# Seven block products for the second linear of ten batches, its h in two loads, and the degrees one burst sooner

## The chip, the cores and the metric

The kernel runs on one core of one Trainium2 chip, as one program with one launch. The metric is the device time of that launch in microseconds (us). All data are float32. The core has five engines with queues of their own: TensorE (PE), VectorE (DVE), ScalarE (ACT), GpSimd (POOL) and SyncE (SP), which here only issues DMAs.

## The reference, cut to what matters

There are two layers over x of 16 batches, 1024 nodes and 256 channels. The first is an attention layer with a graph term; the second aggregates over the graph and applies two linears, each followed by a batch norm over all batches and nodes. The change is in the second linear of the second layer (512 features to 256) and, for one small step, in the node degrees.

```python
def _L1_gnn_ref(features, A, W1, b1, g1, be1, W2, b2, g2, be2):
    ...
    A_norm = A + jnp.eye(n, dtype=A.dtype)
    deg = jnp.sum(A_norm, axis=0) + jnp.sum(A_norm, axis=1) - jnp.diagonal(A_norm)
    dinv = jax.lax.rsqrt(deg)
    A_hat = A_norm * dinv[:, None] * dinv[None, :]
    agg = jnp.einsum('nm,bmd->bnd', A_hat, features)
    x = agg.reshape(-1, d)
    h = jax.nn.relu(_batchnorm(x @ W1.T + b1, g1, be1))
    out = h @ W2.T + b2
    out = _batchnorm(out, g2, be2)
    return out.reshape(b, n, -1)
x = _layernorm(x + _L0_gnn_ref(x, L0_gnn_para, adj, L0_gnn_kv_w), axis=-1)
x = _layernorm(x + _L1_gnn_ref(x, adj, L1_gnn_W1, ..., L1_gnn_be2), axis=-1)
```

## The kernel before

The kernel has four stages in order of time. The order of the work on PE, ACT and DVE is written out by hand in all four (the manual schedules opened at L1158 and L1321); the queues of SP and POOL are ordered by the framework's scheduler, and each is worked off in order.

1. Attention, to about 1698 us. It runs in units of one batch, one pair of heads, one half of the queries and 128 keys; two units make a burst, 16 bursts a batch. In the last batch, work of the second layer is hung on the bursts by their number, in the table `last` (L1193 to L1205): transposing the adjacency (bursts 0 to 7), `degrees` (L1095, burst 9), transposing the weights (10, 11), the first two scalings of the adjacency (12). `degrees` adds up row and column sums on DVE, takes the inverse root on POOL (L589), writes it to DRAM and loads it back as a row on all partitions (L1102, L1104, both in SP's queue). `scale_adjacency` (L1112, DVE) needs that row, and the running sums of the softmax (L955, L957) queue behind it on DVE.

2. Aggregation and the first linear, about 1698 to 2291 us. The products of blocks are made by seven multiplications instead of eight (`products`, L631): from blocks A11..A22 and B11..B22, four sums of the left blocks (`left_sums`, L685) and four of the right (`right_sums`, L691) are formed, and seven products p1, p6, p2, p7, p5, p4, p3 accumulate in three PSUM banks a, b and c. p1 is copied to SBUF by ACT (L650); p6 and p7 plus p1 give the sums u2 and u3 on DVE (L642 with a bias, L640 without); p2 completes output block 0 on ACT (L663); p5 plus u3 gives block 3 (L673), p4 in bank b plus p1 block 2 (L642), p3 in bank c plus u2 block 1 (L681), all on DVE. A bank is added to by a later product (p7 and p4 in b, p2 in a, p3 in c) only when it has been read after the earlier one. The result h (16 batches of 512 x 1024) goes to DRAM (L1415, L1506).

3. The second linear, 2291 to 2511 us, in 16 passes of one batch. `load_h` (L1531, SP) loads one h of 2 MB into one of two 16 KB-a-partition buffers (`hl`), two batches ahead: it starts when PE has finished with the batch whose buffer it takes. ACT applies batch norm and relu in place to the four 128 x 1024 blocks of the next batch (`scale_shift1`, L1482). PE makes 16 products per batch, two blocks of outputs c by four blocks of features k by two halves of the nodes (L1553); a float32 product of 128 x 512 stands in the profile as two matmul instructions. DVE adds the bias into `o2T` in SBUF, where all 16 outputs stay (L1580), and takes statistics of the PSUM tile (L1584). `batchnorm` (L1295) adds the bias to the mean afterwards.

4. The second batch norm, the residual, the layer norm and the output, 2511 to 2605 us. It loads the first layer's results again (`xf`): three batches into the pool `xp`, four into the pool `hl` in two pairs (`load_x1_pair`, L1602), and further ones as buffers come free.

Of the kernel before, what the change touches and what calls it, by code (L numbers as in the profile page):

```python
# [10 lines left out]
F32 = mybir.dt.float32  # L11
I32 = mybir.dt.int32
AF = mybir.ActivationFunctionType
ALU = mybir.AluOpType
# [4 lines left out]
P = 128  # L19
HALF = 512  # L20
# [495 lines left out]
def fast_path(  # L516
# [19 lines left out]
    nc = tc.nc  # L536
    B, N, C = x.shape
    H = 4
    D = C // H
    NCH = N // P  # L540
    CC = C // P
    FH = W1.shape[0]
    HC = FH // P
# [16 lines left out]
    def tile_s(name):  # L560
        return psum["s"].tile([P, N], F32, tag="s", name=name)
# [7 lines left out]
    x1_d = [dram.tile([P, NCH, C], F32, tag=f"x1_{b}", name=f"x1_{b}") for b in range(B)]  # L569
# [115 lines left out]
    def left_sums(eng, S, a11, a12, a21, a22):  # L685
        eng.tensor_tensor(S[0], a21, a22, ALU.add)
        eng.tensor_tensor(S[1], S[0], a11, ALU.subtract)
        eng.tensor_tensor(S[2], a11, a21, ALU.subtract)
        eng.tensor_tensor(S[3], a12, S[1], ALU.subtract)
# [12 lines left out]
    cols = {}  # L702
# [24 lines left out]
    with (  # L727
# [297 lines left out]
        def run(fs, k):  # L1025
            for f, a in fs[:k]:
                f(*a)
            del fs[:k]
# [129 lines left out]
        with tc.manual_schedule(engines={mybir.EngineType.PE, mybir.EngineType.Activation, mybir.EngineType.DVE}):  # L1158
# [33 lines left out]

            last = {u: [(transpose_adjacency, (u, h)) for h in (0, 1)] for u in range(NCH)}  # L1193
            for u, todo in (
                (1, (load_weights,)), (6, (load_x1l, 0)), (9, (degrees,)),
                (10, (transpose_weights, 0)), (11, (transpose_weights, 1)),
                (12, (add_identity,)), (12, (scale_adjacency, 0)), (12, (scale_adjacency, 1)),
            ):
                last.setdefault(u, []).append((todo[0], todo[1:]))
# [92 lines left out]

    w1T, w2T = wl["w1T"], wl["w2T"]

    def batchnorm(stats, gamma, beta, k, name, eng=nc.gpsimd, bias=None):  # L1295

        mv = const.tile([P, k, 2], F32, name=f"{name}_mv")
        sg = const.tile([P, k], F32, name=f"{name}_sg")  # L1300
        sh = const.tile([P, k], F32, name=f"{name}_sh")

        def coefficients(j):
            g, s = sg[:, j : j + 1], sh[:, j : j + 1]
            nc.vector.bn_aggr(mv[:, j, :], stats[:, j].rearrange("p a s -> p (a s)"))
            eng.tensor_scalar(g, mv[:, j, 1:2], EPS, None, ALU.add)
            rsqrt(g, g, 0.0)
            if bias is not None:
                eng.tensor_tensor(
                    mv[:, j, 0:1], mv[:, j, 0:1], bias[:, j : j + 1], ALU.add  # L1310
                )
            eng.tensor_tensor(g, g, gamma[:, j : j + 1], ALU.mult)
            eng.tensor_tensor(s, mv[:, j, 0:1], g, ALU.mult)
            eng.tensor_tensor(s, beta[:, j : j + 1], s, ALU.subtract)

        return coefficients, sg, sh
# [8 lines left out]
    with (  # L1325
# [6 lines left out]
        def bank(name):  # L1332
            return ps8.tile([P, HALF], F32, tag="bank", name=name)

        def temps(k):
            return lambda key, name: strt.tile([P, HALF], F32, tag=f"{key}{k}", name=f"{key}_{name}")
# [144 lines left out]
        def scale_shift1(h, k):  # L1481
            nc.scalar.activation(  # L1482
                h, h, AF.Relu, bias=sh1[:, k : k + 1], scale=sg1[:, k : k + 1]
            )
# [27 lines left out]

    with tc.tile_pool(name="hl", bufs=2) as hl, tc.tile_pool(name="o2p", bufs=1) as o2p:
        o2T = [
            o2p.tile([P, CC, N], F32, tag=f"o2_{b}", name=f"o2_{b}") for b in range(B)
        ]
# [3 lines left out]
        def load_x1(b, pool, tag):  # L1522
            xf[b] = pool.tile([P, NCH, C], F32, tag=tag, name=f"xf_{b}")
            nc.sync.dma_start(xf[b], x1_d[b])

        coefficients2, sg2, sh2 = batchnorm(
            bn2_st, cols["g2"], cols["be2"], CC, "bn2", nc.vector, cols["b2"]
        )
        hs_of = {0: h0}

        def load_h(b):  # L1531
            ht = hl.tile([P, HC, N], F32, tag="hl", name=f"hl_{b}")
            nc.sync.dma_start(ht, h_d[b])
            hs_of[b] = [ht[:, k, :] for k in range(HC)]

        load_h(1)
        for b in range(B):
            if b + 2 < B:
                load_h(b + 2)
            if b + 1 < B:  # L1540
                for k in range(HC):
                    scale_shift1(hs_of[b + 1][k], k)
            h = hs_of.pop(b)
            pss = [tile_s(f"po2_{b}_{c}") for c in range(CC if b < B - 1 else CC - 1)]
            last_ps = [tile_o(f"po2_last_{half}") for half in range(2 if b == B - 1 else 0)]

            def half_ps(c, hs):
                if last_ps and c == CC - 1:
                    return last_ps[0 if hs == H0 else 1]
                return pss[c][:, hs]  # L1550

            def mm(c, k, hs):
                nc.tensor.matmul(  # L1553
                    half_ps(c, hs), w2T[:, k, c * P : (c + 1) * P], h[k][:, hs],
                    start=(k == 0), stop=(k == HC - 1),
                )

            if b == 0:

                for ks in (range(HC // 2), range(HC // 2, HC)):  # L1560
                    for c in range(CC):
                        for k in ks:
                            for hs in (H0, H1):
                                mm(c, k, hs)
            for c in range(CC):
                last = b == B - 1 and c == CC - 1
                if b:
                    for k, hs in (
                        [(k, hs) for hs in (H0, H1) for k in range(HC)] if last
                        else [(k, hs) for k in range(HC) for hs in (H0, H1)]  # L1570
                    ):
                        mm(c, k, hs)
                if last:
                    for hs in (H0, H1):
                        nc.scalar.activation(
                            o2T[b][:, c, hs], half_ps(c, hs), AF.Identity,
                            bias=cols["b2"][:, c : c + 1],
                        )
                else:
                    nc.vector.tensor_scalar(  # L1580
                        o2T[b][:, c, :], pss[c], cols["b2"][:, c : c + 1], None, ALU.add
                    )
                for half, hs in enumerate((H0, H1)):
                    nc.vector.bn_stats(bn2_st[:, c, 2 * b + half, :], half_ps(c, hs))  # L1584
                if b == B - 1:
                    coefficients2(c)
            if b >= B - 3:
                load_x1(b - (B - 3), xp, "x")

# [6 lines left out]
        with (  # L1596
            tc.tile_pool(name="ps_held", bufs=3, space=PSUM) as ps_held,
            tc.tile_pool(name="ps_sum", bufs=2, space=PSUM) as ps_sum,
        ):
            pairs = {}  # L1600

            def load_x1_pair(b):  # L1602

                pairs[b] = hl.tile([P, 2, NCH, C], F32, tag="hl", name=f"xf_{b}_{b + 1}")
                for i in range(2):
                    xf[b + i] = pairs[b][:, i]
                    nc.sync.dma_start(xf[b + i], x1_d[b + i])

            load_x1_pair(3)
            load_x1_pair(5)  # L1610

            def scale_shift(b, cs=range(CC)):
                for c in cs:
# [72 lines left out]
            def finish(b, *coeffs):  # L1686
                xt, hx = xf.pop(b), held.pop(b)
                y = o2T[b].rearrange("p c n -> p (c n)").rearrange("p (n c) -> p n c", c=C)
                last = b == B - 1
                for n in (0, 1, 2, 3) if last else (0, 1):  # L1690
                    rstd, nmr = coeffs[n // 4]
                    nc.vector.tensor_scalar(
                        y[:, n, :], xt[:, n, :], rstd[:, n : n + 1], nmr[:, n : n + 1],
                        ALU.mult, ALU.add,
                    )
                for n in (4, 5, 6, 7) if last else (4, 5, 6, 7, 2, 3):
                    rstd, nmr = coeffs[n // 4]
                    nc.scalar.activation(
                        y[:, n, :], hx[:, (n - 4) * C : (n - 3) * C] if n >= 4 else xt[:, n, :],
                        AF.Identity, bias=nmr[:, n : n + 1], scale=rstd[:, n : n + 1],  # L1700
                    )
                dst = out[b].rearrange("(n p) c -> p n c", p=P)
                if last:
                    nc.sync.dma_start(dst[:, M0, :], y[:, M0, :])
                    nc.scalar.dma_start(dst[:, M1, :], y[:, M1, :])
                elif b >= B - 4:
                    nc.sync.dma_start(dst[:, M1, :], y[:, M1, :])
                    nc.sync.dma_start(dst[:, M0, :], y[:, M0, :])
                else:
                    nc.sync.dma_start(dst, y)  # L1710
                if b in (4, 6):
                    load_x1_pair(b + 6)
                elif b + 7 < B and not 3 <= b < 7:
                    load_x1(b + 7, xp, "x")

            add_x1(0, 2)
            add_x1(0, 3)
# [56 lines left out]
```

## Time and profile before

| | |
|---|---|
| runs | 2607.45, 2608.11, 2610.22 us, median 2608.11 |
| the profiled execution | 2607.23 us, of which 2605.1 us are the span of the core's instructions |
| PE busy | 2560.0 us, 98% of the span |
| DVE, ACT, POOL busy | 58%, 46%, 14% |
| granted TensorE clock | 0.998 |
| second linear, 2291.4 to 2511.3 us | PE busy throughout |

How to read it. The page gives the busy time of each engine, then the costliest groups of instructions: line of the kernel, engine, operation, tiles written and read, count, busy time and the mean duration of one, and behind the last bar how long the engine stood idle just before them and what ended that. A timeline gives start, duration and the same description for single instructions or runs of like ones; when its engine was idle before, the idle time and what ended it follow in brackets. The chain of waits is the sequence of work that ended last, followed back from the end. Consecutive instructions of an engine overlap at their edges, so the distance between two starts, and not the duration, says how fast a queue is worked off.

### The profile page before, as it was taken

Reading aid. Unit: us, or ns where it says so; the run is one execution under the profiler, and the core shown is the slowest. Engines: PE = TensorE matmul, PEld = TensorE weight load, DVE = VectorE, ACT = ScalarE, POOL = GpSimd, SP = SyncE. Lnnn points to the kernel's source line nnn. Section 1 sums busy time; section 2 is a strip of 40 time slices with the busy share of each in tenths; the row PEclk is TensorE's granted clock in tenths of the full one; section 3 lists DMA queues with packets and bytes.
Section 4 is the critical chain, followed back from the end, with each engine's and each line's share of the span. In section 5 each row is a group of like instructions: output and inputs, shape, how many; then the busy total and the mean of one; then the engine's idle time right before and its main releaser. Section 6 shows DMA issues by size and latency. Waiting matters only on the chain.

```text
span 2605.1 us, 32348 instructions
## 1 busy us (share of the span) xinstructions
PE 2560.0 (98%) x13158; PEld 1126.9 (43%) x13158; DVE 1515.6 (58%) x1974; ACT 1201.7 (46%) x1479; POOL 355.8 (14%) x420
## 2 busy tenths in 40 slices
PE   9999999999999999999999999999999999999997
PEld 4443443444434434444444344444444444444455
DVE  5375665655656556556565566675655656443368
ACT  6365564664655646646556464621101111043358
POOL 0010110101101001011010010232211222000026
PEclk9999999999999999999999999999999999999999
DMA  4001101011011010110110101022212222254449
GB/s 145 1 10 42 33 10 41 17 26 33 10 41 34 9 42 10 33 33 10 42 34 9 42 3 48 10 81 97 93 69 93 85 97 77 102 208 161 149 170 345
DMA packets 134622, 168.97 MB, mean 65 GB/s; under 512 B 86848, under 2 KB 120128, under 8 KB 124096
## 3 DMA queue, kind: packets, MB, share of 16 engines
q1 hardware_dynamic: 129104, 115.95, 14.4%
q0 software_dynamic: 4832, 50.34, 4.6%
q8 instruction: 105, 1.72, 0.3%
q10 hardware_dynamic: 528, 0.52, 0.1%
q14 instruction: 53, 0.43, 0.1%
HBM read 99.36 MB, written 67.44 MB: 64 GB/s over the span
## 4 chain that ended last, share of the span: by engine, by line
PE 86%; DVE 9%; ACT 3%; issue 1%; DMA 1%; POOL 0%; DVEq 0%; POOLq 0%; ACTq 0%
PE ps L926 16%; PE pg L829 16%; PE po L947 16%; PE po L1553 8%; PE pv L879 5%; PE b_agg L1371 4%; PE c_agg L1371 4%; PE pk L866 3%; PE a_agg L1371 2%; PE b_h L1403 2%; PE c_h L1403 2%; PE pxT L790 1%; PE a_h L1403 1%; PE den L977 1%; PE pagg L1139 1%; PE pg L851 1%
## 5 line engine op out<-in xcount | busy, mean ns | idle before, releaser
L931 ACT ACTIVATE p<-ps 128x1024 f32<-128x1024 f32 x512 | 496.8, 1024 | 186.0 <-PE ps L926 155.3
L957 DVE TENSOR_TENSOR acc<-acc,p 128x1024 f32<-128x1024 f32 x384 | 485.7, 1265 | 122.6 <-ACT p L931 94.1
L926 PE MATMUL ps<-qT,kT 64*64 64x512 f32 x4096 | 490.8, 592 | 0.7 <-DVE qT L838 0.3
L947 PE MATMUL po<-p,v 64*64 64x512 f32 x4096 | 488.2, 589 | 1.1 <-ACT p L931 1.1
L829 PE MATMUL pg<-wg,x 128*128 128x512 f32 x960 | 420.9, 594 | 0.0
L947 PEld LDWEIGHTS po<-p,v 64*64 64x64 f32 x4096 | 159.8, 133 | 281.7 <-issue 270.2
L1013 POOL TENSOR_TENSOR x<-x,o 128x512 f32<-128x512 f32 x64 | 122.2, 1909 | 1165.9 <-DVE o L1008 1165.9
L829 PEld LDWEIGHTS pg<-wg,x 128*128 128x128 f32 x960 | 178.9, 190 | 221.5 <-issue 208.5
L926 PEld LDWEIGHTS ps<-qT,kT 64*64 64x64 f32 x4096 | 152.0, 133 | 281.5 <-issue 250.2
L1553 PE MATMUL po<-hl,w12T 128*128 128x512 f32 x496 | 213.1, 592 | 0.8 <-ACT hw L1497 0.8
L838 DVE SCALAR_TENSOR_TENSOR qT<-pg,para_s 128x1024 f32<-128x1024 f32 (+1 forms) x34 | 39.2, 1161 | 238.2 <-PE pg L829 235.0
L819 DVE SCALAR_TENSOR_TENSOR wg<-wg,adj_s 128x1024 f32<-128x1024 f32 x128 | 162.1, 1278 | 19.6 <-ACT wg L815 19.6
L810 ACT ACTIVATE wg<-crow,ccol 128x1024 f32<-128x1024 f32 x128 | 147.2, 1150 | 6.5 <-DMA crow<-c 5.8
L1553 PEld LDWEIGHTS po<-hl,w12T 128*128 128x128 f32 x496 | 94.2, 190 | 119.8 <-issue 116.0
L815 ACT ACTIVATE wg<-wg 128x1024 f32<-128x1024 f32 x128 | 136.2, 1065 | 1.8
L1482 ACT ACTIVATE hl<-hl,bn_sh,bn_sg 128x1024 f32<-128x1024 f32 x64 | 74.1, 1228 | 132.7 <-DMA hl<-h 131.3
L879 PE MATMUL pv<-kvw_s,xT 128*128 128x256 f32 x512 | 126.8, 390 | 6.7 <-ACT kT L870 6.7
L965 DVE TENSOR_TENSOR oT<-po,oT 128x512 f32<-128x512 f32 x64 | 44.3, 692 | 145.8 <-ACT oT L964 145.8
L866 PE MATMUL pk<-xT,kvw_s 128*128 128x512 f32 x256 | 121.9, 598 | 3.3 <-ACT v L884 3.3
L1580 DVE TENSOR_SCALAR o<-po,col_b 128x1024 f32<-128x1024 f32 x31 | 39.8, 1284 | 136.8 <-PE po L1553 136.8
L624 ACT ACTIVATE x<-x,nm_l,rs_l 128x256 f32<-128x256 f32 x128 | 64.8, 587 | 110.3 <-POOL nm_l L620 110.3
L841 ACT ACTIVATE qT<-qT 128x1024 f32<-128x1024 f32 (+1 forms) x34 | 34.1, 1007 | 175.9 <-DVE qT L838 175.9
(182 smaller groups left out, 2759.1 us busy)
## 6 DMA issues: line engine op xcount, KB each, us to landing
h<-hw POOLq DMA_DIRECT2D x16, 2048.0 KB, 6.9
hl<-h SPq DMA_DIRECT2D x15, 2048.0 KB
x<-x POOLq DMA_DIRECT2D x16, 1024.0 KB, 4.2
x1l<-x SPq DMA_DIRECT2D x16, 1024.0 KB
xf<-x SPq DMA_DIRECT2D x16, 1024.0 KB
x<-in_x_dram SPq DMA_DIRECT2D x15, 1024.0 KB
out_dram<-o SPq DMA_DIRECT2D x12, 1024.0 KB
crow<-c SPq DMA_DIRECT2D x15, 512.0 KB
```

The source lines that it names most:

```text
L810: nc.scalar.activation(w, s["crow"], AF.Abs, bias=s["ccol"][:, n : n + 1])
L815: nc.scalar.activation(w, w, AF.Tanh, scale=0.5)
L819: nc.vector.scalar_tensor_tensor(w, w, 1.0, adj_s[:, n, :], op0=ALU.subtract, op1=ALU.mult)
L829: nc.tensor.matmul(s["pg"][:, hs], xt[:, n, c * P : (c + 1) * P], s["wg", n][:, hs], start=(n == 0), stop=(n == NCH - 1),)
L866: nc.tensor.matmul(ps, kvw_s[:, c, kc * P : (kc + 1) * P], s["xT"][:, c, hs], start=(c == 0), stop=(c == CC - 1),)
L879: nc.tensor.matmul(pt[:, j * C : (j + 1) * C], s["xT"][:, c, n * P : (n + 1) * P], kvw_s[:, c, C : 2 * C], start=(c == 0), stop=(c == CC - 1),
L926: nc.tensor.matmul(ps[kh * D : (kh + 1) * D, hd * HALF : (hd + 1) * HALF], kT[r, pr, ks], qT[r, pr, qh * HALF : (qh + 1) * HALF], start=Tr ...
L931: nc.scalar.activation(p, ps, AF.Exp)
L947: nc.tensor.matmul(g["po"][kh][hd * D : (hd + 1) * D, :], s["v"][r, m, h * D : (h + 1) * D], p[r, hd * HALF : (hd + 1) * HALF], start=(m = ...
L957: nc.vector.tensor_add(g["acc"], g["acc"], p)
L1371: nc.tensor.matmul(ps, left, right, start=(start and i == 0), stop=(i == NCH // 2 - 1), skip_group_check=True,)
L1553: nc.tensor.matmul(half_ps(c, hs), w2T[:, k, c * P : (c + 1) * P], h[k][:, hs], start=(k == 0), stop=(k == HC - 1),)
```

## The change

- Batches 1 to 10 of the second linear (`SEVEN`) go through `products` too. The left blocks are the blocks of W2 transposed, with sums `w2S` made once on POOL in a buffer of the pool `xp`; the right blocks are feature halves by node halves of h. Every product is two 128 x 128 by 128 x 512 matmuls (i = 0, 1). Batches 0 and 11 to 15 stay as they were.
- The four right sums of a batch, each of two 128 x 512 parts, are made on DVE (`h_sums`) in the space of the outputs of batches 12 to 15, which are not written yet; odd and even batches alternate. The temporaries p1, u2 and u3 lie in the space of the next batch's output.
- h comes in two loads of 1 MB, features k = 0, 2 and k = 1, 3, into four buffers of half the size; from batch 2 on, a load is one batch ahead in the program. ACT scales in the order 0, 2, 1, 3.
- The statistics are taken from `o2T`, with the bias in it, so `batchnorm` adds no bias.
- In the last stage four single loads take the place of the two pairs.
- `degrees` is hung on burst 8 of the last batch.

```diff
-                (1, (load_weights,)), (6, (load_x1l, 0)), (9, (degrees,)),
+                (1, (load_weights,)), (6, (load_x1l, 0)), (8, (degrees,)),
...
-            if bias is not None:
-                eng.tensor_tensor(
-                    mv[:, j, 0:1], mv[:, j, 0:1], bias[:, j : j + 1], ALU.add
-                )
...
-    with tc.tile_pool(name="hl", bufs=2) as hl, tc.tile_pool(name="o2p", bufs=1) as o2p:
+    with tc.tile_pool(name="hl", bufs=4) as hl, tc.tile_pool(name="o2p", bufs=1) as o2p:
...
         def load_h(b):
-            ht = hl.tile([P, HC, N], F32, tag="hl", name=f"hl_{b}")
-            nc.sync.dma_start(ht, h_d[b])
-            hs_of[b] = [ht[:, k, :] for k in range(HC)]
+            parts[b] = [hl.tile([P, 2, N], F32, tag="hl", name=f"hl_{b}_{i}") for i in range(2)]
+            for i in range(2):
+                nc.sync.dma_start(parts[b][i], h_d[b][:, i::2, :])
+            hs_of[b] = [parts[b][k % 2][:, k // 2, :] for k in range(HC)]
+        SEVEN = range(1, B - 5)
+        w2S = xp.tile([P, 4, 2, P], F32, tag="x", name="w2S")
+        K0, K1 = slice(0, HC // 2), slice(HC // 2, HC)
+        left_sums(
+            nc.gpsimd, [w2S[:, i] for i in range(4)],
+            w2T[:, K0, C0], w2T[:, K1, C0], w2T[:, K0, C1], w2T[:, K1, C1],
         )
+        def h_sums(b, i, later):
+            t = parts[b][i]
+            T = [o2T[B - 4 + 2 * (b % 2) + j // 2][:, i, (j % 2) * HALF : (j % 2 + 1) * HALF]
+                 for j in range(4)]
+            b11, b12, b21, b22 = t[:, 0, H0], t[:, 0, H1], t[:, 1, H0], t[:, 1, H1]
+            if not later:
+                nc.vector.tensor_tensor(T[0], b12, b11, ALU.subtract)
+                nc.vector.tensor_tensor(T[1], b22, T[0], ALU.subtract)
+            else:
+                nc.vector.tensor_tensor(T[2], b22, b12, ALU.subtract)
+                nc.vector.tensor_tensor(T[3], b21, T[1], ALU.subtract)
+        def linear2_seven(b):
+            X = parts[b]
...
+            def mm(k, ps, start):
+                for i in range(2):
+                    left, right = {
+                        1: (w2T[:, i, C0], X[i][:, 0, H0]),
+                        2: (w2T[:, 2 + i, C0], X[i][:, 1, H0]),
+                        3: (w2S[:, 3, i, :], X[i][:, 1, H1]),
+                        4: (w2T[:, 2 + i, C1], T(3, i)),
+                        5: (w2S[:, 0, i, :], T(0, i)),
+                        6: (w2S[:, 1, i, :], T(1, i)),
+                        7: (w2S[:, 2, i, :], T(2, i)),
+                    }[k]
+                    nc.tensor.matmul(
+                        ps, left, right, start=(start and i == 0), stop=(i == 1),
+                        skip_group_check=True,
+                    )
...
+            if b in SEVEN:
+                nxt = b + 1
+                if b > 1:
+                    load_h(nxt)
+                p1, p6, p2, p7, p5, p4, p3 = linear2_seven(b)
+                p1()
+                h_sums(b, 1, True)
+                run(rest, 1)
+                p6()
+                run(rest, 1)
+                p2()
+                run(rest, 1)
+                for k in (0, 2):
+                    scale_shift1(hs_of[nxt][k], k)
+                p7()
+                statistics2(b, 0)
+                p5()
+                for k in (1, 3):
+                    scale_shift1(hs_of[nxt][k], k)
+                if nxt in SEVEN:
+                    h_sums(nxt, 0, False)
+                p4()
+                if nxt in SEVEN:
+                    h_sums(nxt, 1, False)
+                p3()
+                if nxt in SEVEN:
+                    h_sums(nxt, 0, True)
+                rest = [(statistics2, (b, i)) for i in (3, 2, 1)]
+                if nxt not in SEVEN:
+                    run(rest, 3)
+                    load_h(nxt + 1)
+                continue
...
-                    nc.vector.bn_stats(bn2_st[:, c, 2 * b + half, :], half_ps(c, hs))
+                    nc.vector.bn_stats(bn2_st[:, c, 2 * b + half, :], o2T[b][:, c, hs])
...
+            if b == 0:
+                for i, later in ((0, False), (1, False), (0, True)):
+                    h_sums(1, i, later)
...
-            load_x1_pair(3)
-            load_x1_pair(5)
+            for b in range(3, 7):
+                load_x1(b, hl, "hl")
...
-                if b in (4, 6):
-                    load_x1_pair(b + 6)
-                elif b + 7 < B and not 3 <= b < 7:
-                    load_x1(b + 7, xp, "x")
+                if b + 7 < B:
+                    load_x1(b + 7, *((hl, "hl") if 3 <= b < 7 else (xp, "x")))
```

## The prediction, on record before the changed kernel ran

> **What bounds the kernel now.** I read the page's engine shares first, then the costliest groups.
>
> ```profile
> PE 2560.0 (98%) x13158; PEld 1126.9 (43%) x13158; DVE 1515.6 (58%) x1974; ACT 1201.7 (46%) x1479; POOL 355.8 (14%) x420
> ...
> L1553 PE MATMUL po<-hl,w12T 128*128 128x512 f32 x496 | 213.1, 592 | 0.8 <-ACT hw L1497 0.8
> ...
> L1482 ACT ACTIVATE hl<-hl,bn_sh,bn_sg 128x1024 f32<-128x1024 f32 x64 | 74.1, 1228 | 132.7 <-DMA hl<-h 131.3
> ```
>
> PE has almost no gaps. In the second linear 496 instructions took 213.1 us with 0.8 us idle before them: 0.4293 us each, or 0.8585 for a product (two instructions), 13.74 for a batch's 16. The time by stretches, asked for one batch, shows the others:
>
> ```profile
> 2401.30:2415.00 13.70, 13.70 (x33) 6.08 (x32) 4.97 (x6) 4.63 (x4) 0.00 (x0) 1.00 0.42 155
> ```
>
> Columns: stretch and length, busy PE, weight loads, DVE, ACT, POOL, clock, DMA share, GB/s. DVE and ACT are a third busy, POOL does nothing, DMA runs at 42%. So a product removed is worth its 0.86 us until DVE, which takes over much work, becomes the slower ring. The timelines of DVE price that work; the first fence is without POOL work, the second beside POOL's sums L686 to L689.
>
> ```profile
> 1716.47 0.68 DVE L696 TENSOR_TENSOR aT<-ahT,aT 128x512 f32<-128x512 f32 x1
> 1717.07 0.68 DVE L693 TENSOR_TENSOR aT<-ahT 128x512 f32<-128x512 f32 x1
> 1717.78 0.69 DVE L694 TENSOR_TENSOR aT<-ahT,aT 128x512 f32<-128x512 f32 x1
> 1718.39 0.68 DVE L695 TENSOR_TENSOR aT<-ahT,ahT 128x512 f32<-128x512 f32 x1
> ```
>
> ```profile
> 2131.77 1.64 DVE L694 TENSOR_TENSOR tT<-agg,tT 128x512 f32<-128x512 f32 x1
> 2133.33 1.75 DVE L695 TENSOR_TENSOR tT<-agg 128x512 f32<-128x512 f32 x1
> ```
>
> A free sum holds the queue for 0.605 us start to start (0.715 where the next one reads it: 1717.07 to 1717.78), a disturbed one for 1.6. How fast PE takes up after DVE:
>
> ```profile
> 1775.72 0.75 DVE L642 SCALAR_TENSOR_TENSOR u_h<-b_h,col_b,p_h 128x512 f32<-128x512 f32 x1 [0.28 <-ACT hw L663]
> ```
>
> ```profile
> 1776.53 1.12 PE L1403 MATMUL b_h<-tT,wS 128*128 128x512 f32 x2 [1.85 <-DVE u_h L642]
> 1777.49 3.60 PE L1371 MATMUL a_agg<-ahT,x1l 128*128 128x512 f32 x8
> ```
>
> The sum ended at 1776.47; the next product follows at 1777.49, one product (0.86) after 1776.63: 0.16 after the release. The other way, b_h started at 2124.51, its slot ended at 2125.37, and DVE read it at 2125.58: 0.21. Loads, from the timelines of SP and ACT:
>
> ```profile
> 2401.62 82.72 SPq L1533 DMA_DIRECT2D hl<-h  x7
> ```
>
> ```profile
> 2409.99 4.63 ACT L1482 ACTIVATE hl<-hl,bn_sh,bn_sg 128x1024 f32<-128x1024 f32 x4 [9.31 <-DMA hl<-h]
> ```
>
> A 2 MB load is issued 0.3 after PE leaves the buffer and used 8.4 later. For the degrees, the chain of waits:
>
> ```profile
> 1672.54 8.42 DMA dinv<-dg
> 1680.97 5.02 DMA dinv_row<-dinv
> ...
> 1696.15 1.03 ACT p L931
> 1697.23 1.09 PE po L947 x8
> ```
>
> [...]
>
> **The change part by part.**
>
> *PE.* Ten batches lose two products each: 20 x 0.8585 = 17.17 us off. At full pace a batch is 14 x 0.8585 = 12.02.
>
> *DVE's ring, batches 2 to 10.* Per batch DVE has eight sums, five reads of PSUM (L642 0.66 start to start, L673/L681 0.605) and four statistics (2.46 for four, so 0.595 each): 10.6 us with two dependent pairs. The order has waits, so I follow one turn from the start of u3 at t: u3 0.66 and a statistic fit before p5 is done, at t+1.72 (p5 follows p7 at once); block 3 0.605, two sums 1.32, block 2 0.66, two sums 1.32, block 1 0.605, four sums 2.42, a statistic 0.595: u2 starts at t+9.24, is there 0.75 later, PE starts p7 0.16 on, runs 1.72, and DVE sees it after 0.21: t+12.08. That is 0.06 over PE's 12.02; block 3 waits for two engines, which costs the first linear's u2 0.06 (0.27 instead of 0.21). I take 12.12, 0.1 over: nine batches +0.9. Bounds: 0 if PE sets the pace; +5 if every start is 0.64, on the way to L642's 0.66 (some ten sums and reads in the turn).
>
> *The first turn.* Six sums for batch 1 stand on DVE behind batch 0's last bias and statistics. With 0 at PE's end of batch 0: bias from 0.21, sums from 2.60; the two T1 end at 4.01 and 5.33. p6, due at 1.72, gets its first half going at 4.17 (2.45 late), the second at 5.49 (0.46 more). u2 waits behind four more sums until 7.66, ends at 8.41, and p7, due at 8.07, starts at 8.57: 0.50. Together +3.4.
>
> *Loads.* Half the bytes each. [...] DVE asks for the parts at 9.4 and 11.4: nothing. If both landed at 8.4, the second part's sums would slip from 11.4 to 13.1, and p7 by 1.8 in every second turn: 0.9 a batch, +8. On SP, xf_0 now stands behind both first h pairs; that queue waits for PE's end of batch 0 there as before. The last stage's single loads are issued no later than the pairs: nothing.
>
> *ACT.* 4 x 1.15 + 0.5 (L650) + 0.6 (L663) = 5.7 of 12.0, and p1's copy needs to be done one product later: hidden.
>
> *POOL.* w2S puts four ops ahead of the write of h 14: at wS's 1.02, 0.72, 1.70, 1.59 it is 5.0, from 2275.2 (PE's last read of the buffer) to 2280.3, and its next work before was at 2282.9: hidden; beyond that it would delay the batch-norm coefficients one for one.
>
> *Degrees.* On DVE they move ahead of two pairs of statistics and one sum of 128x1024: 1667.8 instead of 1670.0. The small DMA goes out once the three before it in SP's queue have, at 1671.5 instead of 1672.5: 1 us. DVE waited 0.97 for the row, and PE 1.11 for ACT behind DVE at 1697.23: 0.9 off; bounds 0 and 1.1.
>
> *Bias and statistics.* One 0.08 step less at the end: 0.1 off. Reading them from SBUF (0.675) or PSUM (0.685) is equal.
>
> Sum: -17.17 + 0.9 + 3.4 - 0.9 - 0.1 = -13.9. From the profiled execution (2607.23, of which 2605.1 are span): 2593.3. The median of the runs is 0.9 higher; I forecast **2594.2**.
>
> **The rivals.** *DVE dearer* (0.22): waits of sums on two engines cost starts; +1 to +6 on the forecast, about 2598. For it: the ring is already at its limit. *Loads land together* (0.10): 2594.2 + 8 = 2602. For it: both go down one queue at once, and DMA had 42% use[...]. *Slower* (0.08): the sums, in the stage's SBUF space and beside loads, run at the disturbed 1.45 (mean of the four tT rows, 1.08 to 1.61): eight times 0.84 makes the turn 18.9; ten turns lose 68, 2662. It decides from a turn of 13.5, where the 13.9 are gone: 0.17 more per sum. Against: POOL idle. *Does nothing* (0.05): another wait, such as buffers tied by false dependences, hands back the 14: 2608.
>
> **How the numbers follow.** Forecast 0.55 (2592 to 2596.5), the rivals as given. A measurement tells about 0.2% (5.2 us). Faster: 0.55 + 0.22 + 0.10 = 0.87; same 0.05; slower 0.08. The range 2592 to 2602.5 holds the first three; its lower end is the forecast without the ring's 0.9 and with a shorter first turn, its upper end the loads' case.
>
> **What would show it.** Right: distance between a batch's first products 12.0 to 12.2; PE waits on DVE of about 3 us at batch 1's p6; sums at 0.68; no PE gap at the burst of 1697. Wrong: DVE without gaps while PE waits in each batch; ACT's scalings of k = 0, 2 starting later than 7 us into a batch; sums over 0.8 us.

## The result, and the profile after

The changed kernel takes 2595.95 us (median of six runs, 2594.79 to 2597.05), the kernel before 2607.90 beside it (2607.22 to 2610.22): ratio 0.9953, 95% interval 0.994 to 0.9966, so 12 us or 0.5% faster. The profiled execution took 2594.79, its span is 2592.7 instead of 2605.1.

The page first, its line of PE, DVE, ACT and POOL:

```profile
PE 2544.9 (98%) x13118; PEld 1119.8 (43%) x13118; DVE 1573.9 (61%) x2082; ACT 1214.5 (47%) x1499; POOL 358.9 (14%) x424
```

PE issues 40 instructions less, which is 20 products of two instructions each, and DVE 108 more. PE is at 98% as before: it still sets the end. The groups of the second linear (line, operation, count, busy us, mean ns, idle time before them and what ended it):

```profile
L1648 PE MATMUL po<-hl,w12T 128*128 128x512 f32 x176 | 76.0, 593 | 0.8 <-ACT hw L1492 0.8
...
L1477 ACT ACTIVATE hl<-hl,bn_sh,bn_sg 128x1024 f32<-128x1024 f32 x64 | 75.6, 1231 | 37.5 <-DMA hl<-h 35.5 <-POOL bn_sh L1309 1.3
...
L1574 PE MATMUL b_o<-o,w2S 128*128 128x512 f32 x80 | 39.0, 608 | 2.9 <-issue 2.4 <-DVE o L1551 0.3 <-DVE o L642 0.2
```

The 496 instructions of the old form are down to 176. ACT's waits for h fell from 131.3 to 35.5 us. The 2.9 us before `b_o<-o,w2S` are new, and the timeline of PE shows that they lie in one place, batch 1:

```profile
2304.75 1.88 PE L1574 MATMUL a_o<-hl,w12T 128*128 128x512 f32 x4
2309.05 1.10 PE L1574 MATMUL b_o<-o,w2S 128*128 128x512 f32 x2 [2.42 <-issue]
2310.40 1.13 PE L1574 MATMUL b_o<-o,w2S 128*128 128x512 f32 x2 [0.26 <-DVE o L1551]
2311.36 1.88 PE L1574 MATMUL a_o<-hl,w12T 128*128 128x512 f32 x4
2313.47 1.98 PE L1574 MATMUL b_o<-o,w2S 128*128 128x512 f32 x4 [0.23 <-DVE o L642]
```

T0 to T3 are the four sums of `h_sums`, each in two parts, one for each load. p6 waits for the sums T1 of both parts (2.42 and 0.26), p7 for u2. For the first of these waits the trace names no cause, but T1 of part 0 ends at 2308.94, 0.11 before the product. The brackets add up to less than the delay, since a product of four instructions is drawn 1.88 long where the next starts 1.72 later. The delay is read from starts: in the kernel "together" below, which has none of these waits, batch 1's p4 comes 22.42 us after the stage's first product, here 26.10: the first turn costs 3.68.

From there on the turns are alike. Distances between the p4 of two batches are 12.19 or 12.20, nine times. One turn by engines (stretch, PE, weight loads, DVE, ACT, POOL, clock, DMA share, GB/s) answers to the 13.70 of before:

```profile
2402.38:2414.58 12.20, 12.20 (x30) 5.24 (x29) 10.74 (x17) 5.68 (x6) 0.00 (x0) 1.00 0.54 172
```

DVE is busy for 10.74 of 12.20 and PE looks busy throughout, so this view does not say which of the two sets the turn. The timeline of DVE over that turn does, from one u3 to the next:

```profile
2400.87 0.75 DVE L642 SCALAR_TENSOR_TENSOR o<-b_o,col_b,o 128x512 f32<-128x512 f32 x1 [0.89 <-PE b_o L1574]
2401.53 0.68 DVE L1594 BATCH_NORM_STATS2 bn_st<-o 128x6 f32<-128x512 f32 x1
2402.58 0.69 DVE L673 TENSOR_TENSOR o<-c_o,o 128x512 f32<-128x512 f32 x1 [0.36 <-PE c_o L1574]
2403.19 0.68 DVE L1550 TENSOR_TENSOR o<-hl 128x512 f32<-128x512 f32 x1
2403.98 0.69 DVE L1551 TENSOR_TENSOR o<-hl,o 128x512 f32<-128x512 f32 x1
2404.59 0.75 DVE L642 SCALAR_TENSOR_TENSOR o<-b_o,col_b,o 128x512 f32<-128x512 f32 x1
2405.25 0.68 DVE L1550 TENSOR_TENSOR o<-hl 128x512 f32<-128x512 f32 x1
2406.03 0.69 DVE L1551 TENSOR_TENSOR o<-hl,o 128x512 f32<-128x512 f32 x1
2406.64 0.68 DVE L681 TENSOR_TENSOR o<-c_o,o 128x512 f32<-128x512 f32 x1
...
2409.65 0.68 DVE L1594 BATCH_NORM_STATS2 bn_st<-o 128x6 f32<-128x512 f32 x1
2410.25 0.73 DVE L642 SCALAR_TENSOR_TENSOR o<-b_o,col_b,o 128x512 f32<-128x512 f32 x1
...
2413.06 0.75 DVE L642 SCALAR_TENSOR_TENSOR o<-b_o,col_b,o 128x512 f32<-128x512 f32 x1 [0.89 <-PE b_o L1574]
```

From block 3 (L673) to u2 (2410.25) DVE has no gap, and PE's p7 starts at 2411.04, right behind u2's end at 2410.98. That is the ring of the prediction. From block 3 on the starts are 0.60 to 0.66 apart but for two: a T1 (L1551) starts 0.79 and 0.78 after the T0 (L1550) that it reads. The sums last 0.68 to 0.69.

Loads, from the timeline of ACT (the two scalings of a part in one line; the batch on PE began at 2405.82):

```profile
2412.02 2.37 ACT L1477 ACTIVATE hl<-hl,bn_sh,bn_sg 128x1024 f32<-128x1024 f32 x2
2415.24 2.37 ACT L1477 ACTIVATE hl<-hl,bn_sh,bn_sg 128x1024 f32<-128x1024 f32 x2 [0.84 <-DMA hl<-h]
```

The first part was used 6.2 us after the batch began, the second 9.4, and the scalings are done at 2417.6, ahead of the T1 at 2418.23 that needs the last block.

For the degrees, the chain of waits of the kernel after:

```profile
1671.05 0.46 SPq L1102
...
1680.24 5.32 DMA dinv_row<-dinv
...
1696.79 1.09 PE po L947 x8
```

The small DMA went out 1.49 us sooner than before, the row only 0.73, and PE's gap ahead of 1696.79 is 0.75 us in this execution instead of 1.11.

### The profile page after: what moved, and what is told of

Same layout as the page of the kernel before. It is cut to its first block, busy times and chain, and to the rows that moved or that the text cites. A ratio compares the mean times of both kernels' runs of the same rounds, so it can differ in the third digit from the quotient of the medians.

```text
span 2592.7 us, 32521 instructions
## 1 busy us (share of the span) xinstructions
PE 2544.9 (98%) x13118; PEld 1119.8 (43%) x13118; DVE 1573.9 (61%) x2082; ACT 1214.5 (47%) x1499; POOL 358.9 (14%) x424
## 3 DMA queue, kind: packets, MB, share of 16 engines
q8 instruction: 105, 1.72, 0.3%
## 4 chain that ended last, share of the span: by engine, by line
PE 86%; DVE 9%; ACT 3%; issue 1%; DMA 0%; POOL 0%; SPq 0%; DVEq 0%; POOLq 0%; ACTq 0%
PE ps L926 16%; PE pg L829 16%; PE po L947 16%; PE pv L879 5%; PE b_agg L1366 4%; PE c_agg L1366 4%; PE pk L866 3%; PE po L1648 3%; PE a_agg L1366 2%; PE b_h L1398 2%; PE b_o L1574 2%; PE c_h L1398 2%; PE c_o L1574 1%; PE pxT L790 1%; PE a_h L1398 1%
## 5 line engine op out<-in xcount | busy, mean ns | idle before, releaser
L879 PEld LDWEIGHTS pv<-kvw_s,xT 128*128 128x128 f32 x512 | 92.8, 190 | 50.1 <-ACT kT L870 25.1
L1366 PE MATMUL a_agg<-ahT,x1l 128*128 128x512 f32 x240 | 108.1, 593 | 0.7 <-ACT agg L1146 0.7
L1366 PE MATMUL b_agg<-aT,x1S 128*128 128x512 f32 x240 | 107.9, 592 | 0.0
L650 ACT COPY p_agg<-a_agg 128x512 f32<-128x512 f32 x15 | 8.8, 585 | 183.4 <-PE a_agg L1366 183.4
```

The costliest lines, as they stand in the source:

```text
L879: nc.tensor.matmul(pt[:, j * C : (j + 1) * C], s["xT"][:, c, n * P : (n + 1) * P], kvw_s[:, c, C : 2 * C], start=(c == 0), stop=(c == CC - 1),
L1366: nc.tensor.matmul(ps, left, right, start=(start and i == 0), stop=(i == NCH // 2 - 1), skip_group_check=True,)
```

## The experiments

Times are compared with the kernel before on the same chip. As some of the effects are smaller than the intervals, a second measure is read from the traces: the *stage*, from the first product of the second linear to the first product that needs the final statistics (L1729, after the gap at the head of the last stage). It is 224.81 us before and 212.93 after, 11.88 less.

| run | time, median | before there | ratio, 95% interval | stage | turn |
|---|---|---|---|---|---|
| changed kernel | 2595.95 | 2607.90 | 0.9953 (0.994 to 0.9966) | 212.93 | 12.20 |
| the same again | 2593.42 | 2607.18 | 0.995 (0.9936 to 0.9963) | 212.93 | 12.20 |
| first sums early | 2590.92 | 2606.73 | 0.994 (0.9926 to 0.9953) | 210.17 | 12.19 |
| one statistic behind u2 | 2592.94 | 2606.73 | 0.9948 (0.9934 to 0.9961) | 212.50* | 12.02 |
| one statistic ahead of u2 | 2600.23 | 2606.73 | 0.9975 (0.9965 to 0.9985) | 218.23 | 12.79 |
| five batches | 2602.52 | 2606.73 | 0.9984 (0.9978 to 0.9991) | 221.14* | 12.19 |
| one load | 2597.35 | 2605.95 | 0.9964 (0.9951 to 0.9978) | 215.65 | 12.50 in the mean |
| eleven batches | 2593.19 | 2605.95 | 0.9949 (0.9935 to 0.9963) | 212.54* | 12.19 |
| dependent sums apart | 2593.03 | 2605.95 | 0.9948 (0.9935 to 0.9962) | 211.31 | 12.02 |
| two sums on POOL | 2595.59 | 2605.95 | 0.9958 (0.9943 to 0.9973) | 214.47* | 12.24 in the mean |
| degrees at burst 9 | 2596.15 | 2607.18 | 0.9959 (0.9945 to 0.9972) | 214.08* | 12.20 |
| together | 2586.85 | 2607.18 | 0.9922 (0.9908 to 0.9935) | 205.93 | 12.02 |
| together, last statistics from PSUM | 2586.98 | 2607.18 | 0.9923 (0.991 to 0.9937) | 205.92 | 12.02 |

In the stages with a star PE ran at half its clock for 3.4 us in batch 1, which was not foreseen. It moves batch 1's p4 from 26.10 us behind the stage's first product to between 27.25 and 27.29 (to 26.63 in the run with five batches). This is taken off below and comes back in the last section.

**First sums early.**

```diff
+            if b == 0:
+                for i, later in ((0, False), (0, True), (1, False)):
+                    h_sums(1, i, later)
             for c in range(CC):
...
-            if b == 0:
-                for i, later in ((0, False), (1, False), (0, True)):
-                    h_sums(1, i, later)
```

> The six sums for batch 1 stand ahead of batch 0's bias and statistics on DVE, in its idle time of 8.9 us; nothing is left out. Theory (the first turn is late because these sums are queued behind the last bias and statistics): p6 and p7 of batch 1 come on time, 3.6 us are saved of the 3.7 that p7 was late, about 2592.3 us; the turns stay at 12.20. Rival (batch 1 waits for its h, or for ACT's scaling of it): the sums start no earlier than before, batch 0's bias is held up behind them, and the time stays at 2596 or rises.

The timeline of PE in this kernel:

```profile
2304.45 1.88 PE L1574 MATMUL b_o<-o,w2S 128*128 128x512 f32 x4
2306.17 1.88 PE L1574 MATMUL a_o<-hl,w12T 128*128 128x512 f32 x4
2308.72 1.98 PE L1574 MATMUL b_o<-o,w2S 128*128 128x512 f32 x4 [0.67 <-DVE o L642]
```

p6 waits no longer. p7 does, for 0.67, since the sums now hold up batch 0's first bias by some 2 us (12.80 behind the stage's first product instead of 10.66), and u2 stands behind the biases and statistics. The stage is 2.76 shorter, not 3.6. The queue behind batch 0's last bias is the cause of the first stall; what remains is the same queue, a step later.

**One statistic behind u2, and one ahead of it.** The first:

```diff
                 h_sums(b, 1, True)
-                run(rest, 1)
                 p6()
-                run(rest, 1)
+                run(rest, 2)
                 p2()
```

> In each of the ten batches one statistic moves from ahead of u2 to behind it on DVE; nothing is left out. Theory (DVE's ring from u3 to u2, 12.20 us, sets the turn): the ring falls by 0.6 to 11.6, PE's 12.02 sets the turn, nine turns save 0.18 each: -1.6 us, about 2594.3. Rival (the turn of 12.20 is PE's own products and restarts): the turn stays at 12.20, 2596.

The second has `run(rest, 2)` ahead of `p6()` and none behind it.

> In each of the ten batches one more statistic stands ahead of u2 on DVE, taken from behind it; DVE's work is the same, nothing is left out. Theory (DVE's ring sets the turn): each turn takes 0.6 more, 12.80, nine turns +5.4 us, about 2601.4. Rival (PE sets the turn): 12.20 as before, 2596.

The turn fell to 12.02 and rose to 12.79. Without the 1.19 at half clock the first stage is 211.31, 1.62 less; the second is 5.30 more, nine times 0.59. 12.02 is PE's own 14 products of 0.8585: below that nothing more can be had from DVE. So DVE's ring sets the turn of the changed kernel, and it is over PE's pace by 0.18.

**Five batches.** `SEVEN = range(1, B - 10)`.

> Five batches instead of ten are done by seven products; nothing is left out. Theory (each such batch saves two products, 1.72 us, and gives back 0.18 where a turn follows; the first turn costs 3.7 once): five times 1.72 lost, five turns of 0.18 saved, +7.7 us, about 2603.6, with the first turn's stall as it was. Rival (the gain is not in the products but in something that is had once, such as the earlier degrees or the shorter loads): about 2596.

The stage is 221.14, less 0.53 at half clock 220.61: 7.68 more. The gain is in the products, batch by batch; the first turn's stall is there as before, once.

**Eleven batches.** `SEVEN = range(1, B - 4)`.

> Eleven batches instead of ten are done by seven products; nothing is left out. Theory: two products less, one more turn at 12.20: -1.72 + 0.18 = -1.5 us. Rival (the eleventh finds its sums' or temporaries' space still in use and waits): no gain, or a loss of up to a turn's difference.

212.54 less 1.19 is 211.35, 1.58 less, ten turns of 12.19. The times themselves (0.9949 and 0.9953) can't tell this from the changed kernel.

**Dependent sums apart.** The sums go in the order T0, T2, T1 of part 0, block 2, T0 of part 1, T3 of part 0, T1 of part 1.

```diff
...
-                    h_sums(nxt, 0, False)
+                    h_sums(nxt, 0, False, (0, 2, 1))
                 p4()
                 if nxt in SEVEN:
-                    h_sums(nxt, 1, False)
+                    h_sums(nxt, 1, False, (0,))
+                    h_sums(nxt, 0, False, (3,))
+                    h_sums(nxt, 1, False, (1,))
                 p3()
-                if nxt in SEVEN:
-                    h_sums(nxt, 0, True)
```

> The same eight sums in another order on DVE, so that none follows the one that it reads; nothing is left out. Theory (a sum that reads its neighbour's result starts 0.785 after it instead of 0.605, twice in a turn): the ring shortens by 0.36 to 11.84, PE's 12.02 sets the turn, nine turns save 0.18 each, -1.6 us. Rival (the 0.18 is a wait for ACT's scaling or for PE, not for the neighbour): the distance stays with the same sum, 12.20 and no change.

The timeline of DVE in this kernel (all sums have one line, L1551):

```profile
2398.76 0.75 DVE L642 SCALAR_TENSOR_TENSOR o<-b_o,col_b,o 128x512 f32<-128x512 f32 x1 [1.10 <-PE b_o L1571]
...
2401.09 1.28 DVE L1551 TENSOR_TENSOR o<-hl 128x512 f32<-128x512 f32 x2
2402.29 0.68 DVE L1551 TENSOR_TENSOR o<-hl,o 128x512 f32<-128x512 f32 x1
...
2403.55 0.68 DVE L1551 TENSOR_TENSOR o<-hl 128x512 f32<-128x512 f32 x1
2404.15 1.28 DVE L1551 TENSOR_TENSOR o<-hl,o 128x512 f32<-128x512 f32 x2
...
2407.76 0.73 DVE L642 SCALAR_TENSOR_TENSOR o<-b_o,col_b,o 128x512 f32<-128x512 f32 x1
```

Each sum starts 0.60 after the one before it, the T1 too, as soon as another stands between it and its T0. From u3 (2398.76) to u2 (2407.76) it is 9.00 instead of the 9.38 between 2400.87 and 2410.25 in the changed kernel. The turn is 12.02 and the stage 1.62 less. The 0.18 over PE's pace is a matter of neighbours that read each other.

**One load.** h in one load of 2 MB into two buffers, with the pairs of the last stage restored for the larger buffers:

```diff
...
-            parts[b] = [hl.tile([P, 2, N], F32, tag="hl", name=f"hl_{b}_{i}") for i in range(2)]
-            for i in range(2):
-                nc.sync.dma_start(parts[b][i], h_d[b][:, i::2, :])
+            t = hl.tile([P, HC, N], F32, tag="hl", name=f"hl_{b}")
+            nc.sync.dma_start(t, h_d[b])
+            parts[b] = [t[:, i::2, :] for i in range(2)]
...
```

> h comes in one 2 MB load per batch again instead of two of 1 MB; sums and products are as they were, nothing is left out. Theory (the first half lands early enough only because it is a load of its own): ACT's scaling of k = 0, 2 starts some 9 us into a batch instead of 6, part 1 is scaled at about 13.5 to 14 where DVE asks for it at 11.6, p7 slips by about 2 in every second turn, +7 to +10 us, 2603 to 2606. Rival (both halves of a pair land together anyway): 2596, no change.

The timeline of ACT in this kernel (the batch on PE began at 2381.97):

```profile
2390.45 4.64 ACT L1477 ACTIVATE hl<-hl,bn_sh,bn_sg 128x1024 f32<-128x1024 f32 x4 [2.39 <-DMA hl<-h]
```

The timeline of DVE:

```profile
2392.85 0.69 DVE L1551 TENSOR_TENSOR o<-hl,o 128x512 f32<-128x512 f32 x1 [0.26 <-ACT hl L1477]
...
2395.11 0.69 DVE L1551 TENSOR_TENSOR o<-hl,o 128x512 f32<-128x512 f32 x1 [0.31 <-ACT hl L1477]
```

And that of PE, at the next p7:

```profile
2400.12 1.98 PE L1574 MATMUL b_o<-o,w2S 128*128 128x512 f32 x4 [0.27 <-DVE o L642]
```

ACT starts 8.5 after the batch began, as expected, and DVE now waits for it. But it waits at the T1 only, and for 0.3: T0 needs one block of its part, T1 the second, 1.15 later, and ACT scales at about the pace at which DVE asks. The stage is 2.72 longer, not 7 to 10. The mechanism is there, but the size expected was about three times too large: expectation and prediction both asked for a whole part at its first sum.

**Two sums on POOL.** `nc.gpsimd` instead of `nc.vector` for T2 and T3 of part 1.

> Two of the eight sums of each batch (T2 and T3 of part 1) are done by POOL instead of DVE; nothing is left out. Theory (the sums are at 0.68 only because POOL is idle): DVE's sums and reads beside POOL's take 1.0 to 1.6, some three or four of them a turn, +0.3 to +0.8 each less the 1.21 taken off DVE; the turn is about 13, some +9 us. Rival (in this stage's space the two engines don't disturb each other): DVE's ring is 11.0, PE sets the turn at 12.02, -1.6 us.

The timeline of DVE in this kernel:

```profile
2392.47 1.11 DVE L1551 TENSOR_TENSOR o<-hl 128x512 f32<-128x512 f32 x1
2393.72 0.69 DVE L1552 TENSOR_TENSOR o<-hl,o 128x512 f32<-128x512 f32 x1
2394.33 0.68 DVE L681 TENSOR_TENSOR o<-c_o,o 128x512 f32<-128x512 f32 x1
2394.93 1.45 DVE L1554 TENSOR_TENSOR o<-hl 128x512 f32<-128x512 f32 x1
2396.30 0.68 DVE L1555 TENSOR_TENSOR o<-hl,o 128x512 f32<-128x512 f32 x1
```

And that of POOL:

```profile
2391.77 1.27 POOL L1554 TENSOR_TENSOR o<-hl 128x512 f32<-128x512 f32 x1 [8.16 <-ACT hl L1477]
2394.55 1.27 POOL L1555 TENSOR_TENSOR o<-hl,o 128x512 f32<-128x512 f32 x1 [1.52 <-DVE o L1552]
```

The expected +9 did not come, nor the rival's gain. Each POOL sum lengthens one DVE sum, by 0.46 (1.25 to the next start instead of 0.79) and 0.77 (1.37 instead of 0.60); together 1.23, what DVE was spared. Six of nine turns stay within 0.03 of 12.20 (the others 12.11, 12.30 and 12.47); without the 1.19 at half clock the stage is 0.35 longer. So in this stage's space too a DVE sum beside one of POOL's took longer: 1.11 and 1.45 us, against 0.68 and 0.69 for the others. The size expected was wrong: in the turn shown each of POOL's sums disturbs one instruction, where three or four a turn had been expected.

**The changed kernel again, and the degrees put back.** The first is the changed kernel, the second has `(9, (degrees,))`.

> The changed kernel itself once more, beside the next three on one chip. Its stage from the first product of the second linear to its last is 208 us where PE's clock stays whole; where the clock falls to half behind the first turn's stall of 2.4 us, which four of eight profiled executions with that stall showed, it is up to 1.2 more.

> The degrees alone are put back one burst later; nothing is left out. Theory: PE's gap at the burst of 1697 is 1.11 again, as in the kernel before, where the profiled executions with the earlier degrees show 0 (six of nine), 0.18, 0.45 and 0.75; so +1.0 us on the changed kernel. Rival (the earlier degrees only move the wait to another place): the gap stays below 0.8 and no time is lost.

The timeline of PE with the degrees at burst 9:

```profile
1696.49 1.09 PE L947 MATMUL po<-p,v 64*64 64x512 f32 x8 [1.04 <-ACT p L931]
```

And of the changed kernel again, with burst 8:

```profile
1693.50 2.61 PE L947 MATMUL po<-p,v 64*64 64x512 f32 x20
1696.04 3.27 PE L1139 MATMUL pagg<-ahT,x1l 128*128 128x512 f32 x7
```

The gap is back with burst 9, and absent with burst 8. The times differ by 2.7 us, more than the gap, with overlapping intervals of the ratios; in the profiled execution with burst 9 half the clock took another 1.15 in batch 1 and 1.04 in the last stage (its transposes at 2522.36 come 17.62 behind the end of PE's gap, and 16.58 in the other), and PE was 0.49 later already at 1652.37 (1651.88 in the other). So what the move is worth is read from the gap, about 1.0 us; the times alone don't show it.

**Together.** First sums early, one statistic behind u2, eleven batches, and batch 0's last two statistics handed on:

```diff
...
+                if b == 0 and c == 1:
+                    rest += [(statistics2, (0, 3)), (statistics2, (0, 2))]
+                    continue
                 for half, hs in enumerate((H0, H1)):
                     nc.vector.bn_stats(bn2_st[:, c, 2 * b + half, :], o2T[b][:, c, hs])
```

> Together: batch 1's six sums ahead of batch 0's bias, batch 0's last two statistics behind batch 1's u2, in each batch one statistic moved behind u2, and eleven batches by seven products; nothing is left out. Theory, if the parts add: no stall in the first turn (-3.6), ten turns at 12.02 instead of nine at 12.20 (-1.6), two products less (-1.7): -6.9 us on the changed kernel, and up to 0.6 more on the mean because no gap of 2.4 us is left there for PE's clock to fall in. Rival (one of the three uses the room of another, such as DVE's idle time in the first turn): -5 or less, with a gap left at p7 of batch 1.

The stage is 205.93, 7.00 less, and PE has no gap in batch 1:

```profile
2303.35 1.88 PE L1574 MATMUL a_o<-hl,w12T 128*128 128x512 f32 x4
2305.07 1.88 PE L1574 MATMUL b_o<-o,w2S 128*128 128x512 f32 x4
2306.78 1.88 PE L1574 MATMUL a_o<-hl,w12T 128*128 128x512 f32 x4
2308.50 1.88 PE L1574 MATMUL b_o<-o,w2S 128*128 128x512 f32 x4
```

The parts add: 3.68 for the first turn, 1.62 for nine turns and 1.72 for two products less are 7.02. At 2586.85 it beats the kernel before by 20.3 us and the changed kernel beside it by 6.6.

**Together, last statistics from PSUM.** `half_ps(c, hs)` instead of `o2T[b][:, c, hs]` in the last batch.

> As the last one, but the last batch's statistics are read from PSUM again, as in the kernel before; nothing is left out. Theory (PE's one gap of 3.0 at the head of the last stage, which was two of 1.5 and 1.2 in the kernel before, is where its clock falls to half in five of nine profiled executions, for 1.1 us): the two gaps are back, the clock stays whole there, 0 to 1.1 us less than the last one from one execution to another, 0.5 in the middle. Rival (the clock falls behind the two gaps just as well): no difference.

A miss: the gap at the head of the last stage is 2.90 in one piece, the clock was at half behind it in this very execution, from 2495.88 to 2499.28, and the time is the same. Where the statistics are read from is not what parted the gap in the kernel before; what did was not found.

## Why the prediction was right, and where its sizes were off

The time came 1.75 above the forecast and within its range. The steps can be told apart in the profiled execution, predicted at 2593.3 and measured at 2594.79. In the second linear, two products less in each of ten batches, the first turn and the ring add up to -17.17 + 3.68 + 1.62 = -11.87, against 11.88 measured.

- *PE, -17.17*: right. Fourteen products take 12.02 where DVE lets them, and five batches less cost 7.68, which is five times 1.72 less five turns of 0.18.
- *DVE's ring, +0.9*: the mechanism right, the size off. The turn is 12.20, not 12.12, and nine turns cost 1.62. The term that failed is "0.715 where the next one reads it": it is 0.785 here, twice a turn, 0.14. With it the ring's sum of 12.08 becomes 12.22, where 12.20 was measured. The further 0.04 put in for block 3's wait for two engines did not show: block 3 starts 1.71 after u3, where the sum has 1.72. Taking the pairs apart brought the turn to PE's 12.02. The 0.715 was read in another stage; why it is 0.07 more here stays open.
- *The first turn, +3.4*: right in its order: p6 waits for the T1 of both parts, then p7 for u2; 3.68 in all. The missing 0.3 has two sources in the trace: a statistic that reads the bias's output starts 1.32 after it (2304.95 to 2306.27) where 1.2 was taken, 0.12 more, and T1 behind T0 again, twice 0.07.
- *Loads, nothing*: right in the outcome; how soon a load of half the size lands was the author's estimate. The parts were used 6.2 and 9.4 after the batch began in the turn shown, the first ahead of the second, and DVE did not wait. The first load went out at 2405.20, 0.6 before the batch began and not 0.3 after, since its buffer is free when the first half of p3 (from 2404.10, 0.86 long) is done; it was used 6.8 us later, and the second, issued 0.86 after the first, 9.2 after its issue. One load instead of two costs 2.7. The rival's 8 us for parts that land together was too much, since a sum needs one block of a part and not the whole.
- *ACT and POOL hidden*: right. ACT is busy for 5.68 of a turn, and PE's start of the stage keeps its distance from the aggregation's first product (593.16 before, 593.10 after). The prices for POOL were not met: w2S ran from 2269.69 to 2272.58, 2.9 us and not 5.0, and began before 2275.2, where the prediction had its buffer come free.
- *Degrees, -0.9*: right, though not in the changed kernel's own profiled execution, which gave 0.36: there dinv's DMA took 9.19 instead of 8.43. Of the twelve profiled executions with burst 8 the gap was gone in nine, and 0.18, 0.45 and 0.75 in three.
- *Bias, -0.1*: wrong, 0. The removed step (L1309 of the kernel before, 2514.03) lay in the time that DVE waited for POOL's root (to 2514.77).
- *The rivals*: DVE was dearer, by 0.7 of that rival's +1 to +6, but by sums that read their neighbour and not by waits on two engines. The loads did not land together. The slower one was refuted: sums at 0.68 with POOL idle. The disturbance whose price it took is real where POOL works, as the run with POOL shows, but costs 0.46 to 0.77 for one sum at a time there, not 0.84 for all eight. The rival in which nothing is gained is refuted by the time.

Together the terms are 0.7, 0.3, 0.5 (degrees, in that execution) and 0.1: 1.6, against the 1.5 between 2593.3 and 2594.79. The median is 1.2 above the profiled execution, and the six runs lie at 2594.8 to 2595.3 and at 2596.6 to 2597.1. That fits stretches at half clock as below: the mean clock is 0.998 in the two runs at 2594.79 and 0.996 or 0.997 in the other four, of which the one at 2595.30 is hardly slower. The single runs have no trace that would show where.

## What to carry to other kernels

When work moves from the engine that bounds to another, follow one turn of the other's queue from a value that the first engine waits for to the next such value: what stands ahead of that value is in the ring, what stands behind it is free, and moving one 0.6 us instruction across it was worth 1.6 us over nine turns here. The queue in front of the first turn deserves the same look, for there the new work met the old pass's last work. And where such a queue sets the pace, put an independent instruction between two of which one reads the other: it took the start of the second from 0.79 to 0.60 behind the one before it.

## What the hardware did that was not expected

PE's clock fell to half behind the first turn's stall of 2.42 us. The stretches of the kernel with one statistic behind u2 (columns as above, the clock being the third from the end), in batch 1 and about a turn later; 5 of PE's instructions fall into 3.0 us there against 9 into 3.4:

```profile
2309.80:2312.80 3.00, 3.00 (x5) 1.20 (x4) 1.66 (x3) 0.00 (x0) 0.00 (x0) 0.57 0.00 0
2321.40:2324.80 3.40, 3.40 (x9) 1.52 (x8) 3.40 (x7) 0.59 (x1) 0.00 (x0) 1.00 0.89 267
```

PE counts as busy all the while, so only the clock and the durations tell. It came in five of the ten profiled executions with the first turn's stall, at 0.5 to 1.2 us each, and in seven of the thirteen with the gap of 2.9 to 3.0 at the head of the last stage, mostly at about 1 us. In the changed kernel's own execution it did not come, nor in that of the kernel before, whose gap there was in two pieces of 1.5 and 1.2: from its first rise, 10.62 and 10.80 us into the span, the clock stayed whole until 2580.86 and 2594.69, behind PE's last product.

Half the clock lasted 3.40 to 3.42 us each time (the missing clock sums to 1.70 or 1.71). Where it begins does not go by the stall alone. In the two executions in which it came twice, the two falls are 194.56 us apart, 57 times 3.413: at 2308.76 and 2503.32 with two sums on POOL, at 2310.08 and 2504.64 with the degrees at burst 9. From the first rise of the clock to its fall behind PE's last product it is 2583.889 us in the kernel before and 2570.236 in the changed kernel, 757 and 753 times 3.4133. So in these four executions the changes of the clock lie on steps of 3.413 us, and a gap falls into one step or is shared by two. Here is the same gap of 2.98 us by such steps, first in the kernel with dependent sums apart, counted back from its fall, then in the changed kernel, counted from its first rise:

```profile
2498.88:2502.29 3.41, 0.91 (x8) 0.92 (x9) 1.16 (x6) 2.73 (x4) 0.55 (x1) 1.00 0.98 411
2502.29:2505.71 3.42, 3.42 (x18) 3.42 (x17) 2.46 (x6) 3.42 (x4) 0.00 (x0) 0.50 0.02 7
```

```profile
2498.94:2502.35 3.41, 1.92 (x6) 0.64 (x4) 1.87 (x3) 3.22 (x4) 0.54 (x1) 1.00 0.87 308
2502.35:2505.77 3.42, 1.93 (x17) 1.93 (x18) 1.79 (x6) 2.80 (x4) 0.01 (x1) 1.00 0.73 307
```

In the first, PE is idle for 2.50 of one step, and the next step runs at half the clock. In the second, both steps have 1.49 of idle time, and the clock stays whole. In twelve executions a fall or the first rise tells where the steps lie. There, by the brackets of PE's timelines from batch 0 to the head of the last stage, the clock fell behind all nine steps with 2.16 to 2.91 us of idle time, behind three of the six with 1.78 to 1.96, and behind none with 1.64 or less. So what a stall cost beyond its length went with where the steps lay in that execution. On average the stall of 2.4 us cost about half a microsecond more than its length here.

The clock's first rise also makes executions differ where no edit does. In the kernel before it came 10.80 us into the span: PE's instructions of 128 x 512 (L802) start at 8.73, 9.58 and 10.44, 0.85 apart, and from 11.05 on 0.43 apart. In the changed kernel it came at 10.62, and the first transposes behind PE's wait of 0.78 (L790) start at 30.04 us, against 30.13 in the kernel before.
